# A two-layer graph transformer on one core: the bias rows move from accumulating transfers to VectorE, x is loaded once per graph, and the order of all pieces is laid anew

## The chip, the cores and the metric

The kernel runs on one core of one Trainium2 chip. The metric is the device time of one execution in microseconds (us), lower is better. The kernel before takes 3296.09 us as the median of three runs (3287.92 to 3308.08). A second set of numbers comes from one profiled execution: the hardware profiler's record of every instruction and every DMA packet. That execution took 3294.25 us, and its span from the first to the last instruction is 3292.5 us.

## The reference

For each of 32 graphs there is `x` (512 nodes x 256 features, float32) and `adj` (512 x 512, int32). Two layers follow each other, cut here to what matters:

```python
def _L0_gnn_ref(x, adj, ...):
    allowed = (adj > 0) | (jnp.swapaxes(adj, 1, 2) > 0) | eye
    q, k, v = heads of x @ Wqkv.T + bqkv               # 8 heads of 32
    attn = softmax(where(allowed, q * scale @ k.T, -inf))
    x = _layernorm(x + (attn @ v) @ Wo.T + bo, ln1_g, ln1_b)
    ff = relu(x @ W1.T + b1) @ W2.T + b2               # 1024 hidden
    return _layernorm(x + ff, ln2_g, ln2_b)

x = _layernorm(x + _L0_gnn_ref(x, adj, ...), axis=-1)  # layer 0
x = _layernorm(x + _L1_gnn_ref(x, adj, ...), axis=-1)  # layer 1: mask adj != 0, attention, Wo, no MLP
```

All matrices of weights stay in SBUF. The sums that a softmax divides by are taken over 512 keys for each of 8 heads and 512 queries.

## The kernel before

Each graph is an object of class `Graph`, and the work on it is cut into small pieces, each a method that issues one to eight instructions. The nodes lie on the 128 partitions in four chunks. A piece is named here as in the code, with its layer and its index: `scores(1, 3)` is the score matmul of layer 1 for head group 0 (four heads) and key chunk 3, `scores(1, 7)` the one of head group 1 and key chunk 3.

**The order is written out by hand.** Five graphs, `a` to `e`, are in work at the same time. `opening` (L578) starts the first ones, `period` (L1421) is run 26 times, each time one graph further on, and `closing` (L1737) finishes the last ones. Under `tc.manual_schedule()` every engine takes its pieces in just this order; a piece waits by semaphores for what it needs. In one `period`, `a` ends layer 1, `b` is in the second norm and layer 1, `c` in layer 0's sums and MLP, `d` in layer 0's scores, `e` is being loaded. Each queue is in order: a DMA that has to wait on SP holds back all DMAs behind it on SP, and likewise on POOL.

**Attention.** `scores` (TensorE), `exp` (ScalarE), `masked` (VectorE, multiplies by the mask, L410) and `product` (TensorE, with `v`) run for eight k per layer. Each `p(layer, k)` holds 128 keys x 4 heads x 512 queries. The sums of `p` over the keys take this chain, for each head group:

- `pair` (L430, POOL queue): an accumulating DMA adds one `p` tile of 1 MB onto its neighbour.
- `fold` (L433, VectorE): adds the partial sums of key chunks into one tile, `p(layer, 2)` or `p(layer, 3)`.
- `halve` (L438, POOL queue): two accumulating DMAs add partitions 64 to 127 onto 0 to 63 (`P // 2`, 512 KB), then 32 to 63 onto 0 to 31 (`P // 4`, 256 KB); the second waits for the first to land.
- `spread` (L443, SP queue): four DMAs of 64 KB bring the four heads under one another into the tile `part`.
- `blocks` (L471), `reduce` (L477), `invert` (L480), `widen` (L488), `divide` (L492), all on VectorE: transpose, last sum, reciprocal, and the scaling of the context `cT`.

`project` (TensorE) multiplies `cT` by Wo, `add` (L512, VectorE) adds the residual. `stats`, `aggregate`, `root` (POOL, two instructions, L523 and L524), `center`, `affine` (VectorE) and `norm` (ScalarE, L544) are the norms; `hidden`, `relu`, `mlp` the MLP. TensorE writes dense results into PSUM tiles that share three buffers (tag `d`).

**x and the biases.** `load` (L278, SP) brings x of a graph into the tile `x`, 512 KB, and `again` (L281, SP) brings it a second time into `x1`. `bias` (L323) adds a row that is the same for all nodes, three times per graph, each by an accumulating DMA of 512 KB on the POOL queue from SBUF to SBUF: `bias(1)` adds `bov[0]` to `x1`, the residual of layer 0's attention; `bias(0)` adds `be2` to `x`, the residual behind the MLP's norm; `bias(2)` adds `bov[1]` to `x2`, the residual of layer 1.

**The next graph's x, transposed.** `flip` (L336, SP) is a DMA transpose of half a graph's x from HBM into the `v` tile, `sort` (L341, SP) moves its 16-bit halves to their places, `join` (ScalarE, L348) puts them together. `entries` (L290) and `entry` (L293) load the adjacency and its transpose from a bfloat16 copy that `cast` (POOL queue, L284) makes.

The pieces around the sums of layer 1's head group 0 stand so in `period` before:

```python
b.fold(1, 2, 2, 0)
...
b.halve(1, 0, P // 2)
...
e.flip(0); b.bias(2); e.flip(1); e.sort(1, 0, 0)
...
b.halve(1, 0, P // 4); b.spread(1, 0, 1); b.halve(1, 1, P // 2); c.bias(0)
...
b.spread(1, 0, 2); b.halve(1, 1, P // 4); e.sort(0, 1, 0); d.pair(0, 0); b.spread(1, 0, 0); d.pair(0, 2)
b.spread(1, 0, 3); b.blocks(1, 0); b.reduce(1, 0); c.mlp(0); c.hidden(1, 4); c.add(2, 0)
```

Of the kernel before, what the change touches and what calls it, by code (L numbers as in the profile page):

```python
# [14 lines left out]
ALU = mybir.AluOpType  # L15
# [12 lines left out]
def kernel(ctx: ExitStack, tc: tile.TileContext, t: dict, out: bass.AP):  # L28
# [12 lines left out]
    nc = tc.nc  # L41
    x, adj = t["x"], t["adj"]
    B, N, D = x.shape
# [107 lines left out]
    def plain(pools: ExitStack):  # L151
# [35 lines left out]
        class Graph:  # L187
# [6 lines left out]
            def at(self, tag, n, shape, dtype=F32, **kw):  # L194

                key = (tag, n)
                if key not in self.tiles:
                    name = f"{tag}_{self.b}" + ("" if n is None else f"_{n}".replace(", ", "_").strip("()"))
                    pool = small if tag in SMALL else ps_s if tag == "s" else ps_a if tag == "acc" else work
                    self.tiles[key] = pool.tile([P, *shape], dtype, tag=tag, name=name, **kw)  # L200
                return self.tiles[key]
# [78 lines left out]
            def again(self):  # L280
                nc.sync.dma_start(out=self.x1, in_=x[self.b].rearrange("(c p) d -> p c d", p=P))  # L281

# [36 lines left out]
            def bias(self, i):  # L319

                row = (be2, *bov)[i]
                dst = self.x if i == 0 else self.x1 if i == 1 else self.x2
                nc.gpsimd.dma_start(out=dst, in_=row[:, None, :].to_broadcast([P, NQ, D]), accum_op=ALU.add)  # L323
# [254 lines left out]
        def opening(a, b, c, d, e):  # L578

            a.load()  # L580
            a.transpose(0, 1)
            a.transpose_out(0, 1)
            a.transpose(0, 0)
            a.cast()
            a.transpose_out(0, 0)
            a.constants(0, 4)
            a.query_key(0, 1, 0, None)
            a.query_key_out(0, 1, 0, None)
            b.flip(0)
            b.sort(0, 1, 0)  # L590
            a.entries()
            a.entry(1)
            a.query_key(0, 0, 0, None)
            a.query_key_out(0, 0, 0, None)
            a.query_key(0, 1, 1, None)
            a.scores(0, 1)
            a.exp(0, 1)
            a.entry(2)
            a.entry(3)
            a.value(0, 0)  # L600
            a.scores(0, 0)
            a.entry(0)
            a.exp(0, 0)
            a.query_key(0, 0, 1, None)
            a.query_key_out(0, 0, 1, None)
            a.query_key_out(0, 1, 1, None)
            a.masks(0)
            a.scores(0, 2)
            a.exp(0, 2)
# [3 lines left out]
            a.value(0, 1)  # L613
            a.value_out(0, 1)
            a.again()
            a.constants(10, 12)
            a.masked(0, 1)
            a.masked(0, 2)
            a.scores(0, 3)
            a.masks(3)  # L620
            a.value_out(0, 0)
            a.product(0, 0)
            a.exp(0, 3)
            b.cast()
            b.flip(1)
            a.constants(22, 23)
            a.scores(0, 4)
            a.masked(0, 3)
            a.exp(0, 4)
            a.masked(0, 4)  # L630
            a.scores(0, 6)
            a.exp(0, 6)
            a.pair(0, 0)
            a.product(0, 1)
            a.product(0, 2)
            a.pair(0, 2)
            b.sort(0, 0, 0)
            a.constants(8, 10)
            b.sort(0, 1, 1)
            a.scores(0, 5)  # L640
            a.exp(0, 5)
            a.masked(0, 5)
            a.product(0, 3)
            a.context(0, 0)
            a.masked(0, 6)
            b.sort(1, 0, 0)
            a.fold(0, 2, 2, 0)
            a.product(0, 4)
            a.pair(0, 4)
            b.sort(0, 0, 1)  # L650
            b.join(0, 0)
            b.sort(1, 1, 0)
            b.sort(1, 1, 1)
            a.scores(0, 7)
            a.product(0, 5)
            a.product(0, 6)
            a.exp(0, 7)
            a.masked(0, 7)
            a.constants(4, 6)
            b.join(1, 1)  # L660
            b.sort(1, 0, 1)
            b.join(1, 0)
            b.join(0, 1)
            a.once(0)
            b.query_key(0, 0, 0, None)
            b.query_key(0, 1, 0, None)
            b.query_key_out(0, 1, 0, None)
            b.query_key_out(0, 0, 0, None)
            b.scores(0, 3)
            b.exp(0, 3)  # L670
            a.halve(0, 0, P // 2)
            a.halve(0, 0, P // 4)
            b.entry(0)
            a.product(0, 7)
            a.spread(0, 0, 0)
            a.spread(0, 0, 3)
            b.scores(0, 0)
            b.exp(0, 0)
            b.query_key(0, 1, 1, None)
            b.query_key_out(0, 1, 1, None)  # L680
            b.entries()
            a.context(0, 1)
            a.spread(0, 0, 1)
            a.fold(0, 3, 6, 7)
            a.fold(0, 3, 3, 4)
            b.scores(0, 2)
            b.exp(0, 2)
            b.value(0, 0)
            a.halve(0, 1, P // 2)
            a.halve(0, 1, P // 4)  # L690
            a.spread(0, 0, 2)
            a.blocks(0, 0)
            a.reduce(0, 0)
            a.invert(0, 0)
            a.spread(0, 1, 0)
            a.spread(0, 1, 2)
            a.spread(0, 1, 1)
            a.widen(0, 0)
            b.scores(0, 1)
            b.exp(0, 1)  # L700
            b.query_key(0, 0, 1, None)
            a.spread(0, 1, 3)
            b.query_key_out(0, 0, 1, None)
            b.value_out(0, 0)
            b.scores(0, 5)
            a.divide(0, 0)
            a.blocks(0, 1)
            b.value(0, 1)
            b.exp(0, 5)
            a.reduce(0, 1)  # L710
            a.invert(0, 1)
            a.widen(0, 1)
            a.divide(0, 1)
            a.project(0, 0)
            a.constants(6, 8)
            a.once(2)
            a.bias(1)
            a.add(1, 0)
            a.add(1, 1)
            c.cast()  # L720
            a.stats(1, 0)
            b.entry(2)
            b.entry(3)
            a.stats(1, 1)
            a.project(0, 1)
            b.value_out(0, 1)
            a.aggregate(1, 0)
            a.aggregate(1, 1)
            a.root(1, 0, 2)
            b.entry(1)  # L730
            c.flip(0)
            a.center(1, 0)
            a.affine(1, 0)
            a.center(1, 1)
            a.guard(0, 0, 0)
            a.affine(1, 1)
            b.masks(0)
            b.masks(1)
            c.sort(0, 1, 0)
            a.transpose(1, 0)  # L740
            a.transpose_out(1, 0)
            b.scores(0, 6)
            a.hidden(0, 6)
            b.exp(0, 6)
            a.hidden(0, 0)
            a.relu(0, 1)
            a.add(1, 3)
            a.add(1, 2)
            a.relu(0, 0)
            b.load()  # L750
            a.hidden(0, 2)
            a.constants(12, 14)
            a.bias(0)
            a.relu(0, 3)
            a.hidden(0, 4)
            b.masks(2)
            a.relu(0, 2)
            b.masked(0, 2)
            a.relu(0, 4)
            b.masked(0, 0)  # L760
            b.scores(0, 4)
            b.masked(0, 1)
            a.stats(1, 2)
            b.product(0, 0)
            b.pair(0, 0)
            b.masked(0, 3)
            b.product(0, 1)
            a.stats(1, 3)
            b.product(0, 2)
            b.exp(0, 4)  # L770
            a.aggregate(1, 3)
            b.product(0, 3)
            b.pair(0, 2)
            a.aggregate(1, 2)
            a.root(1, 2, 4)
            a.center(1, 2)
            a.affine(1, 2)
            a.relu(0, 6)
            a.relu(0, 7)
            a.relu(0, 5)  # L780
            a.mlp(1)
            a.center(1, 3)
            a.affine(1, 3)
            a.transpose(1, 1)
            b.masked(0, 5)
            a.add(2, 1)
            a.stats(2, 1)
            a.constants(17, 20)
            a.mlp(0)
            b.masked(0, 4)  # L790
            a.add(2, 0)
            a.aggregate(2, 1)
            a.stats(2, 0)
            a.aggregate(2, 0)
            a.transpose_out(1, 1)
            a.hidden(1, 0)
            a.constants(14, 17)
            a.constants(20, 22)
            a.hidden(1, 6)
            c.sort(0, 1, 1)  # L800
            a.center(2, 0)
            a.root(2, 0, 2)
            b.context(0, 0)
            a.relu(1, 1)
            a.affine(2, 0)
            a.center(2, 1)
            a.relu(1, 6)
            a.affine(2, 1)
            b.masked(0, 6)
            a.relu(1, 7)  # L810
            c.flip(1)
            c.sort(1, 1, 0)
            a.hidden(1, 4)
            a.hidden(1, 2)
            c.sort(0, 0, 0)
            b.scores(0, 7)
            a.relu(1, 5)
            a.stats(3, 1)
            a.aggregate(3, 1)
            a.relu(1, 2)  # L820
            c.sort(0, 0, 1)
            a.guard(0, 1, 0)
            a.guard(0, 1, 1)
            a.stats(3, 0)
            b.product(0, 4)
            a.relu(1, 0)
            d.cast()
            a.aggregate(3, 0)
            b.pair(0, 4)
            a.relu(1, 3)  # L830
            a.relu(1, 4)
            a.mlp(3)
            b.fold(0, 2, 2, 0)
            b.halve(0, 0, P // 2)
            b.exp(0, 7)
            b.masks(3)
            a.root(3, 0, 2)
            b.masked(0, 7)
            a.add(2, 3)
            a.stats(2, 3)  # L840
            a.aggregate(2, 3)
            a.center(2, 3)
            a.offset(3, 0, 2)
            a.norm(3, 1)
            a.root(2, 3, 4)
            a.affine(2, 3)
# [2135 lines left out]
```

## Time and profile before

| what | value |
|---|---|
| median of three runs | 3296.09 us |
| profiled execution, its own time | 3294.25 us |
| its span | 3292.5 us |
| granted TensorE clock, mean | 0.961 |
| TensorE (PE) busy | 3032.3 us, 92% |
| VectorE (DVE) busy | 2652.7 us, 81% |
| ScalarE (ACT), GpSimd (POOL) busy | 1760.1 us, 1149.4 us |
| stores of a graph (L576), from 1022.7 to 2531.7 us | 16, so 100.6 us per `period` |

A row of a timeline gives the start, the duration in us, the engine, the line, the operation and its tiles, and in brackets how long the engine had been idle and which event ended that. `p_(1_2_10336` is the tile `p(1, 2)` of a graph, the last number tells buffers apart. "SPq" is a DMA issued on SP; the duration of such a row is that of the issue, not of the transfer. In the view by stretches each engine's busy time is followed by its number of instructions, and behind these stand the granted clock, the mean busy share of the 16 DMA engines (over 1 where packets overlap) and GB/s.

### The profile page before, as it was taken

The page shows a single profiled execution, that of the slowest core. Times are in us where ns is not written, and L with a number is a line of the kernel's source. Part 1 is how long each engine was busy: PE and PEld are TensorE (multiplying, and loading weights), DVE is VectorE, ACT ScalarE, POOL GpSimd, SP SyncE. Part 2 cuts the span into 40 slices and gives each one's busy share as a digit, 9 for nine tenths or more (in the row PEclk, how much of TensorE's full clock was granted, in tenths as well). Part 3 has the DMA queues.
Part 4 walks back from the last instruction along what each step waited for, and adds up shares of the span by engine and source line. Part 5 has one row for each costly group of instructions (what it writes and reads, how often), then busy time and mean ns, then how long its engine had stood idle before and what let it go on. Part 6 is the DMA issues. An engine that isn't in the chain of part 4 may idle for free.

```text
span 3292.5 us, 43923 instructions
## 1 busy us (share of the span) xinstructions
PE 3032.3 (92%) x16242; PEld 1758.3 (53%) x16242; DVE 2652.7 (81%) x3556; ACT 1760.1 (53%) x2111; POOL 1149.4 (35%) x1474
## 2 busy tenths in 40 slices
PE   6998999999999999998999999999999999999988
PEld 2654555555555555555555555555555555555454
DVE  4687988888978888887789778788888897878876
ACT  4445555555655555555556554565555555555543
POOL 1232433343433333323334333343333333343332
PEclk9899999999999999999999999999999999999999
DMA  8898989998888998898988899888999888898862
GB/s 180 145 168 143 161 165 163 173 173 157 159 159 163 175 173 141 158 168 162 173 151 157 161 164 175 157 154 162 164 170 175 161 150 159 162 179 151 154 125 53
DMA packets 364767, 521.93 MB, mean 159 GB/s; under 512 B 161473, under 2 KB 311105, under 8 KB 327745
## 3 DMA queue, kind: packets, MB, share of 16 engines
q0 software_dynamic: 95056, 364.42, 65.5%
q1 hardware_dynamic: 269488, 154.63, 20.9%
q8 instruction: 130, 2.13, 0.3%
q14 instruction: 93, 0.75, 0.1%
HBM read 89.01 MB, written 33.55 MB: 37 GB/s over the span
## 4 chain that ended last, share of the span: by engine, by line
DVE 33%; PE 29%; DMA 16%; SPq 7%; issue 7%; ACT 5%; POOL 2%; DVEq 0%; POOLq 0%; ACTq 0%
SPq L443 5%; PE psF L571 4%; PE psQK_None L383 4%; PE psH L555 3%; PE psO L501 3%; PE psQK L383 3%; PE psV L371 2%; SPq L341 2%; POOL rs L524 1%; PE psT L358 1%; DVE mv L518 1%; POOL rs L523 1%; ACT x L544 1%; DVE x L541 1%; DVE cT L492 1%
## 5 line engine op out<-in xcount | busy, mean ns | idle before, releaser
L555 PE MATMUL psH<-xT,w_L_gnn_W 128*128 128x256 f32 x2048 | 513.3, 411 | 139.7 <-DVE y_(2_0_8655 L512 9.6
L555 PEld LDWEIGHTS psH<-xT,w_L_gnn_W 128*128 128x128 f32 x2048 | 418.6, 207 | 244.1 <-ACT cT L426 20.5
L523 POOL TENSOR_SCALAR rs<-mv 128x2 f32<-128x2 f32 (+1 forms) x320 | 275.2, 860 | 720.1 <-DVE mv L518 694.7
L565 ACT ACTIVATE hT<-psH,c_L_gnn_b 128x256 f32<-128x256 f32 x512 | 217.8, 473 | 468.2 <-PE psH L555 464.1
L571 PE MATMUL psF<-w_L_gnn_W,hT 128*128 128x256 f32 x2048 | 463.8, 382 | 0.0
L571 PEld LDWEIGHTS psF<-w_L_gnn_W,hT 128*128 128x128 f32 x2048 | 381.5, 190 | 95.7 <-ACT hT L565 43.7
L524 POOL TENSOR_TENSOR rs<-rs,neg_half 128x2 f32<-128x2 f32 (+1 forms) x320 | 283.5, 886 | 26.9
L501 PE MATMUL psO<-w_L_gnn_Wo,cT 128*128 128x256 f32 x1024 | 251.7, 400 | 33.4 <-DVE cT L492 33.4
L383 PE MATMUL psQK_None<-xT,w_L_gnn_Wqkv 128*128 128x512 f32 x512 | 243.9, 609 | 4.7 <-DMA w_L_gnn_Wqkv<-in_L_gnn_Wqkv_dram 4.7
L501 PEld LDWEIGHTS psO<-w_L_gnn_Wo,cT 128*128 128x128 f32 x1024 | 202.8, 202 | 84.1 <-DVE cT L492 36.6
L383 PEld LDWEIGHTS psQK_None<-xT,w_L_gnn_Wqkv 128*128 128x128 f32 x512 | 92.6, 191 | 133.8 <-issue 109.4
L358 PEld LDWEIGHTS psT<-ident,x 128*128 128x128 f32 x520 | 59.7, 144 | 129.8 <-ACT x L544 83.0
L371 PE MATMUL psV<-w_L_gnn_Wqkv,xT 128*128 128x256 f32 x512 | 127.4, 392 | 0.0
L358 PE MATMUL psT<-ident,x 128*128 128x128 f32 x520 | 89.6, 292 | 40.3 <-ACT x L544 33.0
L371 PE MATMUL psV<-w_L_gnn_Wv,xT 128*128 128x256 f32 x512 | 124.4, 386 | 0.0
L371 PEld LDWEIGHTS psV<-w_L_gnn_Wqkv,xT 128*128 128x128 f32 x512 | 92.2, 189 | 58.0 <-issue 25.2
L371 PEld LDWEIGHTS psV<-w_L_gnn_Wv,xT 128*128 128x128 f32 x512 | 92.5, 190 | 36.5 <-issue 26.5
L363 ACT COPY xT<-psT 128x512 f32<-128x512 f32 x130 | 75.1, 578 | 60.7 <-PE psT L358 60.7
L323 POOL DMA_DIRECT2D x<-bov x64 | 98.1, 1532 | 3.2 <-PE psT L358 2.1
L348 ACT COPY xT<-kT 128x512 uint16<-128x512 uint16 x124 | 94.2, 765 | 7.0 <-DMA kT<-v 4.7
L389 ACT ACTIVATE qT<-psQK_None,c_L_gnn_bqkv 128x512 f32<-128x512 f32 x64 | 43.9, 688 | 74.0 <-PE psQK_None L383 74.0
L376 ACT COPY v<-psV 128x512 f32<-128x512 f32 x128 | 73.9, 581 | 11.7 <-PE psV L371 11.6
(6836 smaller groups left out, 6570.3 us busy)
## 6 DMA issues: line engine op xcount, KB each, us to landing
x<-in_x_dram SPq DMA_DIRECT2D x64, 512.0 KB, 4.5
x<-bov POOLq DMA_DIRECT2D x64, 512.0 KB, 8.0
code<-in_adj_dram POOLq DMA_DIRECT2D x32, 512.0 KB, 6.6
m<-code SPq DMA_DIRECT2D x32, 512.0 KB, 13.1
x<-s_L_gnn_ln_b POOLq DMA_DIRECT2D x32, 512.0 KB, 9.1
out_dram<-x SPq DMA_DIRECT2D x32, 512.0 KB, 4.6
kT<-v SPq DMA_DIRECT2D x248, 64.0 KB, 5.7
m<-code SPq DMA_TRANSPOSE x128, 4.1
```

Of the source, the lines that this page charges most:

```text
L323: nc.gpsimd.dma_start(out=dst, in_=row[:, None, :].to_broadcast([P, NQ, D]), accum_op=ALU.add)
L348: nc.scalar.copy(words[:, :, h * 2 * P : (h + 1) * 2 * P, w], self.sorted(h)[:, w * ND : (w + 1) * ND, :])
L358: nc.tensor.transpose(ps[:, c, j * P : (j + 1) * P], src[:, 2 * h + j, c * P : (c + 1) * P], ident)
L371: nc.tensor.matmul(ps[:, j, :], xT[:, i, at], proj[layer][0][2][:, i, :], start=(i == 0), stop=(i == ND - 1))
L383: nc.tensor.matmul(ps, w[:, i, c * P : (c + 1) * P], xT[:, i, at], start=(i == 0), stop=(i == ND - 1))
L443: nc.sync.dma_start(out=part[j * HD : (j + 1) * HD, :], in_=self.p(layer, 2 + hg)[:HD, j, :])
L501: nc.tensor.matmul(ps[:, j, :], self.cT(layer)[:, k, at], wo[layer][:, k, :], start=(k == 0), stop=(k == ND - 1))
L523: nc.gpsimd.tensor_scalar(rs, self.mv(n)[:, a:b, 1:2], EPS, None, ALU.add)
L524: nc.gpsimd.tensor_tensor(rs, rs, neg_half[:, a:b, None], ALU.pow)
L555: nc.tensor.matmul(ps[:, j, :], w1[:, c, at], xT[:, c, h * 2 * P : (h + 1) * 2 * P], start=(c == 0), stop=(c == ND - 1),)
L565: nc.scalar.activation(self.hT(h)[:, f, :], ps[:, f % 2, :], AF.Relu, bias=b1[:, f : f + 1])
L571: nc.tensor.matmul(ps, self.hT(h)[:, f, j * P : (j + 1) * P], w2[:, f, :], start=(f == 0), stop=(f == NF - 1))
```

## The change

`again` is gone and `bias` becomes one VectorE instruction on 128 partitions x 1024 elements with the row broadcast. `bias(1)` now writes `x1` from `x`, so x is read from HBM once by `load` (the transposed copy through `flip` stays). A helper also names tiles in another way.

```diff
-            def again(self):
-                nc.sync.dma_start(out=self.x1, in_=x[self.b].rearrange("(c p) d -> p c d", p=P))
...
             def bias(self, i):
 
-                row = (be2, *bov)[i]
+                row = (be2, *bov)[i][:, None, :].to_broadcast([P, NQ, D])
                 dst = self.x if i == 0 else self.x1 if i == 1 else self.x2
-                nc.gpsimd.dma_start(out=dst, in_=row[:, None, :].to_broadcast([P, NQ, D]), accum_op=ALU.add)
+                nc.vector.tensor_tensor(dst, self.x2 if i == 2 else self.x, row, ALU.add)
```

`opening`, `period` and `closing` hold new lists. `period` has the same pieces as before without `again`, in another order and cut at another point of the cycle. Its two DMA queues now read, from the start of the list to its end:

```
SP:   a.spread(1,1,1) a.spread(1,1,0) a.spread(1,1,2) d.sort(0,1,1) d.sort(0,0,0) d.entries d.sort(1,0,1)
      d.load d.sort(1,1,1) d.entry(0) d.entry(2) d.sort(0,0,1) c.spread(0,0,0) c.spread(0,0,2)
      c.spread(0,0,1) c.spread(0,0,3) c.spread(0,1,3) c.spread(0,1,0) c.spread(0,1,2) c.spread(0,1,1)
      d.entry(3) e.entry(1) e.flip(1) e.sort(1,0,0) b.spread(1,0,3) e.flip(0) e.sort(1,1,0) b.spread(1,0,2)
      b.spread(1,0,1) b.spread(1,0,0) e.sort(0,1,0) a.store b.spread(1,1,3)
POOL: c.pair(0,0) b.root(3,0,2) c.pair(0,2) b.root(2,3,4) b.root(3,3,4) b.root(2,2,3) b.root(3,2,3)
      c.halve(0,0,64) b.guard c.pair(0,4) c.halve(0,0,32) c.halve(0,1,64) a.guard a.root(4,2,4) a.root(4,0,2)
      b.guard c.halve(0,1,32) e.cast b.pair(1,0) b.pair(1,2) c.root(1,0,2) c.guard a.guard a.guard b.pair(1,4)
      c.root(1,2,4) b.halve(1,0,64) b.halve(1,0,32) b.halve(1,1,64) b.halve(1,1,32) c.guard b.guard
      c.root(2,0,2)
```

The stretch of the new `period` from layer 1's folds over its end into the next one, where `b` becomes `a`, `c` becomes `b` and `d` becomes `c`:

```python
b.fold(1, 2, 2, 0)
...
d.masks(0); c.affine(1, 2); c.center(1, 3); c.affine(1, 3); b.halve(1, 0, P // 2)
b.fold(1, 3, 6, 7); b.fold(1, 3, 3, 4); b.halve(1, 0, P // 4); b.halve(1, 1, P // 2); b.halve(1, 1, P // 4)
b.product(1, 7); d.masked(0, 0); c.mlp(1); c.add(2, 1); d.masked(0, 1); c.mlp(0); c.add(2, 0)
...
e.flip(1); e.sort(1, 0, 0); b.spread(1, 0, 3); e.flip(0); d.masked(0, 3); e.sort(1, 1, 0)
b.spread(1, 0, 2); d.masked(0, 2); b.spread(1, 0, 1); b.spread(1, 0, 0); b.blocks(1, 0); b.reduce(1, 0)
...
e.sort(0, 1, 0); c.root(2, 0, 2); a.store(); c.affine(2, 0); b.spread(1, 1, 3); d.product(0, 1)
# the next period
a.divide(1, 0); b.affine(2, 1); a.spread(1, 1, 1); a.spread(1, 1, 0); c.product(0, 2); c.pair(0, 0)
a.spread(1, 1, 2); a.blocks(1, 1); b.mlp(3); c.masked(0, 5); a.reduce(1, 1); c.pair(0, 2)
...
a.widen(1, 1); b.mlp(2); c.product(0, 3); a.divide(1, 1); a.project(1, 0)
```

In the middle of the new list, where layer 0's sums end: `c.fold(0, 3, 3, 4)`, `c.bias(0)`, two halves and four spreads, `c.blocks(0, 1)` to `c.divide(0, 1)`, then `c.project(0, 0)`. `b.bias(2)` stands just ahead of that fold, `d.bias(1)` between `b.masked(1, 6)` and `b.fold(1, 2, 2, 0)`.

## The prediction

> **What bounds the kernel now.** I began with the page's busy shares, went on to VectorE's timeline of one `period` (1522 to 1623 us) for its idle times, then to POOL's and SP's timelines for the chain behind the largest of them, and last to stretches of 5 us for the clock.
>
> ```profile
> span 3292.5 us, 43923 instructions
> PE 3032.3 (92%) x16242; PEld 1758.3 (53%) x16242; DVE 2652.7 (81%) x3556; ACT 1760.1 (53%) x2111; POOL 1149.4 (35%) x1474
> q0 software_dynamic: 95056, 364.42, 65.5%
> q1 hardware_dynamic: 269488, 154.63, 20.9%
> ```
>
> TensorE is nearly full; the two DMA queues together keep the 16 engines busy 86% of the time, q0 being all that POOL issues. TensorE's own work per period, from start-to-start times in its timeline: 16 `scores` of 1.07, 16 `product` of 0.95, 8 `hidden` of 1.79, 4 `mlp` of 3.6, 4 `project` of 1.81, 4 `value` of 1.83, 6 full and 4 half `query_key` of 1.82 and 0.93, 4 `transpose` of 0.55: **92.4 us**. The period takes 100.6. The missing 8.2 us are mostly one place:
>
> ```profile
> 1592.53 0.88 POOL L438 DMA_DIRECT2D p_(1_2_10336<-p_(1_2_10336  x1
> 1593.15 1.63 POOL L323 DMA_DIRECT2D x<-bov  x1
> 1600.19 0.88 POOL L438 DMA_DIRECT2D p_(1_2_10336<-p_(1_2_10336  x1 [2.97 <-DMA p_(1_2_10336<-p_(1_2_10336]
> 1604.81 1.33 POOL L323 DMA_DIRECT2D x<-s_L_gnn_ln_b  x1 [1.35 <-issue]
> 1605.91 3.00 SPq L443 DMA_DIRECT2D part_(1_0_10583<-p_(1_2_10336  x2
> 1610.85 3.46 SPq L443 DMA_DIRECT2D part_(1_0_10583<-p_(1_2_10336  x2
> 1621.73 0.71 DVE L471 STREAM_TRANSPOSE sT_(1_0_10663<-part_(1_0_10583 128x512 f32<-128x512 f32 x1 [9.73 <-DMA part_(1_0_10583<-p_(1_2_10336]
> ```
>
> The chain of layer 1's first head group takes 29.2 us from its first `halve` (1592.53) to `blocks` (1621.73), and VectorE stands 9.73 us before `blocks`. `add(2, 0)` stands behind that and frees a PSUM buffer, so TensorE stops too. Both adding rows of `bias` lie inside the chain. What the stretches show of the same place:
>
> ```profile
> 1607.00:1612.00 5.00, 5.00 (x40) 2.61 (x33) 4.86 (x8) 3.58 (x4) 2.05 (x4) 1.00 1.07 169
> 1612.00:1617.00 5.00, 5.00 (x25) 4.41 (x24) 0.01 (x1) 1.74 (x4) 0.73 (x1) 1.00 0.97 145
> 1617.00:1622.00 5.00, 0.48 (x3) 0.08 (x1) 0.27 (x1) 0.84 (x2) 0.00 (x0) 0.75 1.04 209
> 1622.00:1627.00 5.00, 3.14 (x7) 2.52 (x8) 3.65 (x8) 0.00 (x0) 1.34 (x4) 0.50 1.02 181
> ```
>
> TensorE is idle from 1617, the DMA share is 0.97 to 1.07, and after the stop the granted clock is 0.50 for a while: 16 `hidden` matmuls that take 3.62 us elsewhere took 5.11 at 1524.53, behind the same stop. So a stop costs its length and about 1.5 us more.
>
> On this the Trainium skill has a rule (TensorE: Matmul & The Clock Gate, What's actually happening): after an idle window of about 3.4 us the array drops to half rate until it has been busy as long. The row agrees. By the rule a stop of 6 us split into two of 3 would save the 1.5 us; the sum below takes no such saving.
>
> **VectorE's own account** decides the rest. Its work per period: 16 `masked` and 6 `fold` of 2.2, four each of `blocks`, `reduce`, `widen`, `divide` of 0.70, four `invert` of 0.25, `masks` 3.0, 12 `add` and 16 `stats` and 8 `center` of 0.43, 8 `affine` of 0.46, 16 `aggregate` of 0.15, 5 `offset` of 0.13: 85.8 us. Its idle times in that period's timeline: 9.73 at `blocks`, 1.36 for an `exp`, and 1.15, 1.16, 0.94, 0.27 for `root`: 14.6. Together 100.4, the period.
>
> **The change, part by part.** (1) *Three bias adds on VectorE.* No row shows a 128x1024 float32 add. `fold`, with two float32 inputs in SBUF, takes 2.29 for 2048 elements, `divide` 0.69 for 512; between them 1.0 to 1.4, and I take half a `fold`, 1.17. Three make 3.5 us: VectorE 89.3 us of work beside TensorE's 92.4. None of the three waits: x2's transposes and x's load are over 10 us earlier in the new order. At full cover they cost nothing; without cover 3.5 x 26 = 91 us.
>
> The row that speaks against them: `root`'s second instruction has a median of 0.72 us (L524) but took 2.65 at 1533.90, inside a `masked` from 1533.69 to 1535.98. A bias add could hold one `root` by at most its 1.17. In the new order `halve` or `pair` follow each of them on POOL rather than a `root`, so I take 0, with 3.5 per period as the other end. The Trainium skill (SBUF, Who interferes with whom) says just that: a VectorE instruction with two SBUF inputs keeps a GpSimd instruction that reads SBUF waiting until it ends. By its rule alone the three adds would cost POOL up to their whole length, by the order nothing on the path.
>
> (2) *Three accumulating transfers and one load go.* q0 takes 0.655 x 3292.5 = 2157 us for 364.42 MB, 5.9 us per MB; three of 0.524 MB are 9.3 us of the DMA engines' time per period, and `again` at q1's 4.4 us per MB 2.3. These are estimates. The period's DMA load falls from about 0.89 x 100.6 = 89.5 to 78 us. POOL loses three issues of 1.5 us, SP one of 0.6; neither is full. What this buys is shorter landings: a 512 KB `halve` took 5.5 us from issue to landing in layer 0's second group (view of DMA issues for 1520 to 1625) and 7.4 in layer 1's first, four `spread` 2.6 against 7.3.
>
> (3) *The order.* I measure it by the work that each engine has between two pieces of the new list, in the durations above. Two places are tight.
>
> Place one, **layer 0's second group**. From the end of `fold(0,3,3,4)` to `blocks(0,1)` VectorE has 14.1 us of work and some 1.2 idle for a `root`. In the old trace the same chain went from 1556.83 to the last landing at about 1573.8: 17.0 us. So VectorE waits about 1.7 there, and `project(0,0)`, which follows `divide(0,1)` closely, makes TensorE wait about 2 (between 0, if VectorE is ahead, and 4).
>
> Place two, **layer 1's sums**. Let F be the end of `fold(1,2,2,0)`. `halve` 64 and 32: F+11 by layer 0's landings (5.5 and 4.8, plus issues), F+14 by layer 1's old ones. On SP `spread(1,0,3)`, then `flip(0)` with an issue of 2.7 us, a `sort`, three more `spread` (0.65 each when nothing holds them): F+17 to F+20, landing 2.6 us later. VectorE has 19.2 us of work up to `blocks(1,0)`, so it waits 0 to 4 there. The second group's spreads are behind `sort(0,1,0)`, and that waits for `flip(0)` to land (8.2 us after its issue, L336's median): F+20 to F+23, then `store` and four `spread`, landing at F+25 to F+30. VectorE reaches `blocks(1,1)` at F+25.4 plus what it waited before. `project(1,0)` needs VectorE to have finished 12.0 us of the new list when TensorE has done 11.8. From `project(0,0)` to there TensorE has 53.8 us, VectorE 52.6: only 1.2 to spare. With 0.7 of `root` waits and about 3 at the two `blocks`, TensorE waits 2.5 (0 to 7). `add(2,0)` no longer stands behind `blocks(1,0)`: the old stop is gone, and this is what is late next.
>
> **The sum.** 92.4 + 2.0 + 2.5 + 0.6 for a clock that dips now and then = 97.5 us per period against 100.6: 26 x 3.1 = 81 us less. VectorE's account agrees: 89.3, 1.7 and 3 at `blocks`, about 3 for `root`, 0.5 for TensorE. `opening` and `closing` have TensorE lists of the same length to 2 us; they stop in many places (3080 to 3100 has 13.5 busy of 20) and closing gets 17 us more VectorE work beside idle VectorE. I take 0, with 25 either way. 3294.25 - 81 = **3213 us**; the profiled execution lies 2 us under the median of the runs.
>
> **Rivals.**
>
> *TensorE runs through* (B). For it: DMA load falls 13%, and spreads landed in 2.6 us where the engines were less busy. Against it: a flip now sits among the spreads. The period is 92.4 to 94: 26 x 7.3 = 190 less, 3104.
>
> *The wait only changes places* (C). For it: in the trace SP stood 6.8 us before a `sort` until a flip had landed, and such a pair now stands ahead of each group of spreads. If the spreads keep landing in 7 us, the two `blocks` cost VectorE 6 instead of 3 and the period is about 100: 3280.
>
> *VectorE becomes the bound* (D, slower). Place: `blocks(1,0)` and `blocks(1,1)` behind flips and sorts on SP. VectorE has 89.3 us of work; once its idle time is over 11.3 us per period, against 14.6 now, it alone makes the period longer than 100.6. If the whole 14.6 stays, the period is 103.9: 26 x 3.3 = 86 more, 3380. Against it: the bias transfers that shared the chain's stretch are gone.
>
> *The change not doing what it says*: that the order gives nothing by itself and the transfers alone count is inside C.
>
> **How the numbers follow.** Forecast (3150 to 3265) 0.45, B 0.15, C 0.20, D 0.20. The range leaves out the lower half of B and most of D: 3100 to 3330. A measurement of this kernel tells about 1% (33 us) from no change. Faster by over 1%: the forecast, B and a little of C, 0.63; within 1%: most of C, 0.16; slower: D and a remainder, 0.21.
>
> **What would show it.** Stores 97 to 98 us apart. On VectorE no wait over 5 us; `blocks` waits of 1 to 4 at (1,0), (1,1) and (0,1). TensorE waiting at `project` (L501) for `divide` (L492), no longer at `hidden` (L555) for `add` (L512). Bias adds of 1.0 to 1.4 us. DMA share at 0.80 to 0.85. I would be wrong if landings stayed at 7 us, if SP's sorts held the spreads longer than one flip, or if some tile's buffer is now reused so early that a DMA waits for its last reader.

## The result, and the profile after

The changed kernel takes **3405.22 us** (median of four runs, 3402.22 to 3416.09); the kernel before, on the same chip, 3292.65 us (3287.92 to 3308.08). The ratio is **1.034, 95% interval 1.030 to 1.038**: slower, where 3213 was forecast. The profiled execution took 3408.14 us, its mean granted clock is 0.951 (0.961 before). The stores of 16 graphs in the middle of the trace are 104.7 us apart, before 100.5 by the same count. 26 periods of 4.2 us make 109 of the 114 us by which the two profiled executions differ.

The first lines of the page of the changed kernel, its two DMA queues, and two of its costliest groups (number of instructions, then busy time and mean ns of one, then the idle time ahead of the group and what ended most of it):

```profile
span 3406.4 us, 43921 instructions
...
PE 3041.2 (89%) x16242; PEld 1762.2 (52%) x16242; DVE 2764.9 (81%) x3652; ACT 1734.3 (51%) x2111; POOL 1002.4 (29%) x1378
...
q0 software_dynamic: 44368, 314.08, 54.2%
q1 hardware_dynamic: 252592, 137.85, 17.7%
...
L498 PE MATMUL psO<-w_L_gnn_Wo,cT 128*128 128x256 f32 x1024 | 308.8, 456 | 250.0 <-DVE cT L489 249.5
...
L468 DVE STREAM_TRANSPOSE sT<-part 128x512 f32<-128x512 f32 x126 | 89.1, 707 | 322.7 <-DMA part<-p 320.8
```

The two queues carry 67 MB less, as they should, and the engines are less busy with them (72% of a longer span against 86%). TensorE now waits mainly in one group, the matmuls of `project` (now L498): 250 us, for `divide` (L489). VectorE lost 323 us ahead of `blocks` (L468), waiting for `spread`. In the kernel before, `project` (L501) and `hidden` (L555) stood so:

```profile
L501 PE MATMUL psO<-w_L_gnn_Wo,cT 128*128 128x256 f32 x1024 | 251.7, 400 | 33.4 <-DVE cT L492 33.4
L555 PE MATMUL psH<-xT,w_L_gnn_W 128*128 128x256 f32 x2048 | 513.3, 411 | 139.7 <-DVE y_(2_0_8655 L512 9.6
```

The stop at `hidden` is gone, as was forecast (1.8 us of idle time on the new page), but the new one at `project` is larger, and the matmuls of `project` are slower (456 ns on the mean, 400 before). One period of the timeline shows where. L435 is `halve`, L281 `cast`, L440 `spread`, L427 `pair`:

```profile
1611.62 0.82 POOL L435 DMA_DIRECT2D p<-p  x1 [7.89 <-DVE p L430]
...
1617.22 0.87 POOL L435 DMA_DIRECT2D p<-p  x1 [0.40 <-DMA p<-p]
1617.83 0.81 POOL L281 DMA_DIRECT2D code<-in_adj_dram  x1
...
1621.97 6.52 SPq L440 DMA_DIRECT2D part<-p  x4
...
1625.23 0.90 POOL L427 DMA_DIRECT2D p<-p  x1 [6.59 <-DMA part<-p]
1626.94 0.87 POOL L427 DMA_DIRECT2D p<-p  x1 [0.81 <-PE acc L414]
...
1635.92 0.71 DVE L468 STREAM_TRANSPOSE sT<-part 128x512 f32<-128x512 f32 x1 [9.56 <-DMA part<-p]
...
1639.30 5.00 PE L498 MATMUL psO<-w_L_gnn_Wo,cT 128*128 128x256 f32 x14 [8.41 <-DVE cT L489]
...
1678.66 0.71 DVE L468 STREAM_TRANSPOSE sT<-part 128x512 f32<-128x512 f32 x1 [0.65 <-DMA part<-p]
```

This is layer 0's second group. Its four spreads, issued in 2.4 us where nothing holds them, take SP 6.5 us; 3.73 of these are the second one's issue alone. They land 4.71, 8.38, 7.46 and 8.78 us after their issues, the last at 1635.84. The same four in the trace of before:

```profile
1567.88 3.33 SPq L443 DMA_DIRECT2D part_(0_1_10373<-p_(0_3_9959  x4
```

They had landed 2.0 to 3.5 us after their issues, the last at 1572.61, beside one `bias` transfer (issued 1563.77, landing 1571.14). What is new beside them is `e.cast` (issued 1617.83, landing 8.63 us later) and then `b.pair(1, 0)` and `b.pair(1, 2)` (landing 8.35 and 12.62 us after their issues). In the old list `e.cast` stood at the start of the period, and the first of the two pairs was issued (1573.62) when the last spread had landed. The last row of the period above (1678.66) is layer 1's first group, where VectorE waited 9.73 us before: it now waits 0.65. The stop has moved from one group of sums to another.

The stretches of the same place (VectorE's column is the third):

```profile
1629.00:1634.00 5.00, 1.89 (x6) 0.76 (x4) 0.00 (x0) 2.93 (x3) 0.00 (x0) 1.00 1.02 200
1634.00:1639.00 5.00, 0.00 (x0) 0.00 (x0) 2.81 (x5) 0.00 (x0) 0.00 (x0) 0.70 0.87 172
1639.00:1644.00 5.00, 4.70 (x14) 3.81 (x14) 4.08 (x7) 0.00 (x0) 0.00 (x0) 0.62 0.03 7
```

While VectorE and then TensorE stand, the DMA engines are full (1.02, 0.87); when the second pair has landed too, 3.7 us behind the last spread (1639.57), they are empty (0.03). TensorE comes back at a granted clock of 0.62.

### The profile page after: what moved, and what is told of

The parts are those of the page before. It is cut to its first block, busy times and chain, and to the rows that moved or that the text cites. A ratio compares the mean times of both kernels' runs of the same rounds, so it can differ in the third digit from the quotient of the medians.

```text
span 3406.4 us, 43921 instructions
## 1 busy us (share of the span) xinstructions
PE 3041.2 (89%) x16242; PEld 1762.2 (52%) x16242; DVE 2764.9 (81%) x3652; ACT 1734.3 (51%) x2111; POOL 1002.4 (29%) x1378
## 4 chain that ended last, share of the span: by engine, by line
PE 52%; DVE 17%; DMA 15%; issue 6%; SPq 5%; ACT 3%; POOL 2%; DVEq 0%; POOLq 0%; ACTq 0%
PE psH L552 12%; DMA part<-p 10%; PE psF L568 10%; PE s L394 9%; PE acc L414 7%; PE psO L498 7%; DVE p L407 6%; DMA p<-p 5%; SPq L440 5%; DVE p L430 3%; ACT p L403 3%; PE psQK_None L380 2%; PE psV L368 2%; PE psT L355 2%; PE psQK L380 1%
## 5 line engine op out<-in xcount | busy, mean ns | idle before, releaser
L403 ACT ACTIVATE p<-s 128x2048 f32<-128x2048 f32 x512 | 961.3, 1878 | 707.6 <-PE s L394 481.1
L407 DVE TENSOR_TENSOR p<-p,m 128x2048 f32<-128x2048 f32 x512 | 1155.5, 2276 | 59.1 <-ACT p L403 59.0
L394 PE MATMUL s<-qT,kT 32*128 32x512 f32 x4096 | 591.2, 647 | 84.1 <-ACT p L403 75.2
L498 PE MATMUL psO<-w_L_gnn_Wo,cT 128*128 128x256 f32 x1024 | 308.8, 456 | 250.0 <-DVE cT L489 249.5
L414 PE MATMUL acc<-p,v 128*32 128x512 f32 x4096 | 491.8, 601 | 1.6 <-ACT cT L423 1.2
L435 POOL DMA_DIRECT2D p<-p x252 | 212.2, 845 | 861.3 <-DVE p L430 445.6
L430 DVE TENSOR_TENSOR p<-p,p 128x2048 f32<-128x2048 f32 x189 | 430.8, 2280 | 3.7 <-DMA p<-p 2.0
L520 POOL TENSOR_SCALAR rs<-mv 128x2 f32<-128x2 f32 (+1 forms) x320 | 167.6, 524 | 791.1 <-DVE mv L515 781.8
L498 PEld LDWEIGHTS psO<-w_L_gnn_Wo,cT 128*128 128x128 f32 x1024 | 231.4, 234 | 320.9 <-DVE cT L489 261.6
L394 PEld LDWEIGHTS s<-qT,kT 32*128 32x128 f32 x4096 | 161.3, 184 | 369.5 <-ACT p L403 162.9
L468 DVE STREAM_TRANSPOSE sT<-part 128x512 f32<-128x512 f32 x126 | 89.1, 707 | 322.7 <-DMA part<-p 320.8
L427 POOL DMA_DIRECT2D p<-p x189 | 172.4, 913 | 526.8 <-PE acc L414 219.7
L414 PEld LDWEIGHTS acc<-p,v 128*32 128x32 f32 x4096 | 109.5, 109 | 327.8 <-issue 249.4
L521 POOL TENSOR_TENSOR rs<-rs,neg_half 128x2 f32<-128x2 f32 (+1 forms) x320 | 260.7, 815 | 26.8
L512 DVE BATCH_NORM_STATS2 st<-y 128x6 f32<-128x256 f32 x384 | 159.1, 422 | 7.2
```

The source lines that it names most:

```text
L394: nc.tensor.matmul(s[:, j, :], self.kT(layer)[at, hg, kc * P : (kc + 1) * P], self.qT(layer)[at, hg, :], start=True, stop=True,)
L403: nc.scalar.activation(self.p(layer, k), self.at("s", (layer, k), [HPC, N]), AF.Exp, scale=SCALE)
L407: nc.vector.tensor_tensor(p, p, m[:, k % NQ, None, :].to_broadcast([P, HPC, N]), ALU.mult)
L414: nc.tensor.matmul(acc[j * HD : (j + 1) * HD, :], self.v(layer)[:, kc, h * HD : (h + 1) * HD], self.p(layer, k)[:, j, :], start=(kc == 0), ...
L430: nc.vector.tensor_tensor(self.p(layer, dst), self.p(layer, a), self.p(layer, b), ALU.add)
L435: nc.gpsimd.dma_start(out=p[:rows], in_=p[rows : 2 * rows], accum_op=ALU.add)
```

## The experiments

Three theories stood at the start. **Theory 1**: the new order puts `cast`, and then two pairs, beside the spreads of layer 0's second group, on the same DMA engines. **Theory 2**: VectorE, with three adds more, has become the bound. **Theory 3**: the new order as a whole leaves the chains too little time. All ratios are to the kernel before, run on the same chip; the last column is the mean of 16 distances between stores in the middle of one profiled execution.

| run | median us | ratio, 95% interval | us per period |
|---|---|---|---|
| the change | 3405.22 | 1.0339 (1.0296 to 1.0382) | 104.7 |
| cast_late | 3176.53 | 0.9639 (0.9589 to 0.9688) | 96.1 |
| pairs_late | 3312.23 | 1.0060 (1.0038 to 1.0082) | 100.7 |
| no_bias_add | 3370.68 | 1.0233 (1.0188 to 1.0279) | 104.0 |
| old_order_vector_bias | 3215.49 | 0.9765 (0.9708 to 0.9822) | 98.2 |
| old_order_cast_beside | 3217.75 | 0.9767 (0.9727 to 0.9806) | 98.2 |
| new_order_transfer_bias | 3531.77 | 1.0735 (1.0687 to 1.0784) | 108.0 |
| cast_early | 3359.34 | 1.0194 (1.0153 to 1.0235) | 103.0 |
| cast_behind_pairs | 3167.65 | 0.9645 (0.9619 to 0.9672) | 95.3 |
| cast_late_bias1_late | 3131.40 | 0.9488 (0.9446 to 0.9529) | 95.0 |
| casts_late_all | 3110.04 | 0.9487 (0.9440 to 0.9533) | 92.7 |

### One piece moved: the cast

```diff
             c.halve(0, 1, P // 4)
-            e.cast()
...
             c.root(1, 0, 2)
+            e.cast()
```

> The changed kernel with one piece moved in `period`: `e.cast` from behind `c.halve(0,1,32)` to behind `c.root(1,0,2)`, where the trace shows the DMA engines idle (share 0.01 to 0.03). Theory 1, collision on the DMA engines: the four spreads of layer 0's second group share the engines with `cast` and then with two `pair` of 1 MB, so that they land 8.8 us after their issue and not 2.6; without `cast` their issue takes 3.3 us in place of 5.1 and they land 3 to 6 us earlier. TensorE's wait at `project(0,0)` falls from about 9 us to 3 to 6 per period, the time from 3405 to 3260 to 3330. Theory 2, VectorE is the bound with its 3.6 us more work: no change, 3390 to 3410. Theory 3, the order alone leaves the chain of halves and spreads too little time, whatever the engines do: at most 1 us per period, 3380.

It took **3176.53 us**, 229 us less than the change, more than theory 1 had said. The waits between 600 and 2800 us of the changed kernel (total us, number of waits, longest):

```profile
PE psO L498 <- DVE cT L489: 189.8, 22, 12.7
...
DVE sT L468 <- DMA part<-p: 226.9, 40, 13.8
```

and of this one:

```profile
PE s L394 <- ACT p L403: 64.5, 47, 4.7
PE psO L498 <- DVE cT L489: 3.8, 3, 2.2
...
DVE sT L468 <- DMA part<-p: 19.7, 22, 3.4
```

The wait at `project` is all but gone, and the wait at `blocks` with it. The timeline of the same chain:

```profile
1505.48 0.82 POOL L435 DMA_DIRECT2D p<-p  x1 [7.52 <-DVE p L430]
...
1511.50 0.87 POOL L435 DMA_DIRECT2D p<-p  x1 [0.82 <-DMA p<-p]
...
1516.23 2.78 SPq L440 DMA_DIRECT2D part<-p  x4
...
1519.09 0.89 POOL L427 DMA_DIRECT2D p<-p  x1 [6.71 <-DVE p L407]
...
1520.48 0.71 DVE L468 STREAM_TRANSPOSE sT<-part 128x512 f32<-128x512 f32 x1 [0.26 <-DMA part<-p]
```

The four issues take 2.78 us in all, and they are over before the first pair is issued, though the pairs have kept their place in the list. From the end of `fold(0, 3, 3, 4)` (1505.19) to the last landing (1520.40) the chain takes 15.2 us; in the changed kernel the same chain took 24.5 (1611.32 to 1635.84). Theory 3 falls with this as it was put: the order as a whole stays, and one piece moved gives back all that was lost and more.

### The other neighbours: the two pairs

```diff
-            b.pair(1, 0)
-            b.pair(1, 2)
...
             c.root(1, 0, 2)
+            b.pair(1, 0)
+            b.pair(1, 2)
```

> The changed kernel with `b.pair(1,0)` and `b.pair(1,2)` moved in `period` from ahead of the second group's spreads to behind `c.root(1,0,2)`; `cast` stays. Theory 1 (collision): the spreads land after 3 to 5 us, not 8.8, TensorE's wait at `project(0,0)` falls from 9 to about 3 or 4 per period, but `fold(1,2,2,0)` then may wait a few us for the second pair: 3250 to 3340. Theory 2 (VectorE): no change. Theory 3 (order alone): no change or slower, since layer 1's chain starts later.

3312.23 us. The cast is where the change has it, and the second spread's issue still takes 3.3 us (1677.80 in this trace), but the third and fourth, issued behind it, now land in 2.0. The chain takes 18.4 us (1665.45 to 1683.85). Its waits, 600 to 2800 us:

```profile
PE s L394 <- ACT p L403: 100.6, 55, 5.0
PE psO L498 <- DVE cT L489: 43.1, 22, 2.5
...
DVE sT L468 <- DMA part<-p: 99.3, 44, 3.7
DVE p L430 <- DMA p<-p: 88.1, 25, 5.0
```

So the delay has two links. The cast holds back one issue on SP by about 3 us; the pairs are issued meanwhile, and beside them the last three spreads need 7 to 9 us in place of 2 to 5. Taking the second link away costs something new here: the folds wait 88 us for pairs that are now late (last row).

### Is VectorE the bound?

The three adds are left out, so the output lacks the three bias rows:

```diff
-                nc.vector.tensor_tensor(dst, self.x2 if i == 2 else self.x, row, ALU.add)
+                return
...
-                    r = self.x1 if n == 1 else self.x2
+                    r = self.x if n == 1 else self.x2
```

> The changed kernel without the three bias adds: the rows are left out of the computation, `add` of layer 0's attention reads x itself. VectorE has 3.6 us less work per period. Theory 2 (VectorE is the bound): the whole 3.6 x 26 = 95 us go, 3310. Theories 1 and 3 (the wait for the spreads sets the period): only the add that stands ahead of `fold(0,3,3,4)` starts the chain earlier, 1.2 us per period, about 30 us: 3375.

3370.68 us, 34.5 less than the change, where theory 1 had said some 30 and theory 2 had said 95. By the stores the period is 104.0: of 3.66 us of VectorE work, 0.7 came back. TensorE waits as long as ever for `divide`:

```profile
PE psO L498 <- DVE cT L489: 198.1, 22, 12.6
```

Theory 2 falls for the changed kernel. In the changed kernel's period VectorE's idle times in the timeline add up to 15.5 us and its work to the other 89.1, but 9.56 of the idle time is the wait for the spreads.

### The transfers alone, in the old order

Before's lists with the VectorE add and one load; two `bias` pieces in `opening` change places and `closing` loads `d` earlier, so that x is there.

> The kernel before, in its own order, with the bias rows added by VectorE and x loaded once: the first half of the change without the new order (bias keeps its places in the list; for two graphs of `opening` its first two calls are swapped, and one `load` of `closing` takes the place of the second load, so that x1 is made from x before the second row is added to x). Theory 1 (collision): the two bias transfers that ran beside layer 1's chain are gone, the stop of 6.8 us per period shrinks to 2 to 4: 3190 to 3240, so the new order alone cost 170 to 210 us. Theory 2 (VectorE): the added 3.6 us show wholly or in part, 3300 to 3390. Theory 3 gives nothing of its own here: 3290.

3215.49 us: taking the bias and the second load off the DMA engines is worth 2.3% (1.8 to 2.9) with the order left as it was. Beside this run the new order costs 190 us as it was delivered, and it gains 39 with the cast moved (`cast_late`, 3176.53, on the same chip).

### The cast beside the spreads, in the old order

```diff
-            e.cast()
...
             c.halve(0, 1, P // 4)
+            e.cast()
```

> The old order with the bias adds on VectorE (3215.49 us), with one piece moved: e.cast from the start of period to just behind c.halve(0, 1, P // 4), where the new order has it, so beside the four spreads of layer 0's second group; the two pairs of layer 1 stay well behind those spreads. Theory 1 (the transfer of cast holds up the spreads, in any order): the second spread's issue goes from 0.6 to 3-4 us and the last of the four lands 5 to 8 us later than now. But in the old order VectorE reaches blocks(0, 1) 6.4 us after that landing, so most of it is covered: 3215 to 3270. Theory 3 (the new order as a whole is at fault, the cast only a part of it): issues stay at 0.6 and landings at 2.0. If the cast cost its 8 us wherever it stands beside spreads, without regard to cover: 3330 or more.

3217.75 us, no difference. The timelines of POOL, SP and VectorE in this run:

```profile
1534.21 0.79 POOL L281 DMA_DIRECT2D code<-in_adj_dram  x1
...
1538.33 5.75 SPq L440 DMA_DIRECT2D part_(0_1_10357<-p_(0_3_9944  x4
...
1548.70 0.70 DVE L468 STREAM_TRANSPOSE sT_(0_1_10385<-part_(0_1_10357 128x512 f32<-128x512 f32 x1
```

and in the old order without the move:

```profile
1628.82 2.41 SPq L440 DMA_DIRECT2D part_(0_1_11032<-p_(0_3_10619  x4
...
1639.02 0.70 DVE L468 STREAM_TRANSPOSE sT_(0_1_11060<-part_(0_1_11032 128x512 f32<-128x512 f32 x1
```

The first link is there again: the four issues take 5.75 us in place of 2.41, and the last landing is 17.6 us behind the fold's end (1527.83 to 1545.47) in place of 14.5 (1618.14 to 1632.61). But `blocks` comes 20.9 us behind that end in both (no bracket in either row: VectorE didn't wait), and here the pairs are issued only when the spreads have been issued. The new order's list gives the chain some 15 us, the old one 21. The cast's hold on SP is the same in both orders; what it costs is decided by the cover, which is the work that VectorE has meanwhile, and by what POOL issues meanwhile.

### Earlier by one place, later by two

```diff
+            e.cast()
             c.halve(0, 1, P // 4)
-            e.cast()
```

> The new order with e.cast moved by one place only, from just behind c.halve(0, 1, P // 4) to just ahead of it: POOL issues it about 4.5 us earlier, while the first half of the chain is on its way. Theory 1 as it stands (cast against the spreads): the spreads' issues come back to 0.6 us and they land in 2 to 5; the two halves lose some 2 us each; VectorE waits 3 to 7 at blocks(0, 1) in place of 9.6; 3230 to 3340. If what counts is only that the 1.5 MB of the cast and the chain share the engines at some time between fold and blocks: 3390 to 3420, as the changed kernel.

3359.34 us, above what theory 1 had said. POOL's and SP's timelines:

```profile
1600.57 0.64 POOL L281 DMA_DIRECT2D code<-in_adj_dram  x1
1601.19 0.87 POOL L435 DMA_DIRECT2D p<-p  x1
...
1608.20 2.78 SPq L440 DMA_DIRECT2D part<-p  x4
...
1608.73 0.89 POOL L427 DMA_DIRECT2D p<-p  x1 [6.67 <-PE acc L414]
```

SP's issues are free again (2.78), so the hold does belong to the cast. But the second `halve` now lands 6.88 us after its issue, where it took 4.6 alone, and that is enough to bring the last two spreads beside the pair of 1608.73: they land in 7.48 and 8.25 us, and the chain takes 23.4 (1594.83 to 1618.27). From period to period it takes 17.1 to 27.3.

```diff
-            e.cast()
...
             b.pair(1, 2)
+            e.cast()
```

> The changed kernel with e.cast moved by two places on the POOL queue, from ahead of b.pair(1, 0) to behind b.pair(1, 2): still in the same stretch, but issued some 3 us behind the spreads of layer 0's second group in place of 4 us ahead of them. Theory 1, as the last runs narrowed it (the cast holds the second spread's issue on SP for 3 us, and this brings the last two spreads beside the two pairs): issues of 0.6 us, landings of 2 to 3, the wait at blocks(0, 1) gone; only the pairs land later, by at most the cast's own 5 us; 3165 to 3230. If the bytes of cast and pairs in this stretch are what counts, whatever their order: 3300 to 3405.

**3167.65 us**, as good as `cast_late`, with the cast in the same stretch and all the same bytes. The spreads land in 2.0 us and the chain takes 15.0 (median of 16 periods; in the changed kernel the median is 24.6); only the cast itself is slow now, 13.5 us from issue to landing, and nobody waits for it. The bytes in the stretch aren't the cause; which of them stand ahead of the spreads is. Waits of this run, 600 to 2800 us:

```profile
PE s L394 <- ACT p L403: 63.9, 48, 3.9
PE psO L498 <- DVE cT L489: 2.6, 2, 2.3
```

### The accumulating transfers in the new order

`cast_late` with `bias` as three accumulating transfers and `again` in its lists, as in the kernel before.

> The new order with e.cast behind c.root(1, 0, 2) as in the run of 3176.53 us, but with the three bias rows as accumulating transfers on the POOL queue and x loaded a second time (again behind c.spread(0, 1, 1) in period, behind load elsewhere). If the price of the transfers is that of the old order (76 us), about 3252, 3220 to 3290. If the new order leans on VectorE's adds (c.bias(0) now stands between the halves of layer 0's groups, d.bias(1) and b.bias(2) beside folds), over 3290. If the transfers are hidden in this order, 3176 to 3200.

**3531.77 us**, against 3176.53 with the adds: in this order the transfers cost 11%, in the old one 2.4% (1 / 0.9765). POOL's, VectorE's and TensorE's timelines (L323 is `bias`, L438 `halve`, L430 `pair`):

```profile
1546.61 0.89 POOL L430 DMA_DIRECT2D p<-p  x1 [1.46 <-PE acc L417]
1547.19 1.65 POOL L323 DMA_DIRECT2D x<-bov  x1
1548.78 0.90 POOL L438 DMA_DIRECT2D p<-p  x1
1549.31 1.74 POOL L323 DMA_DIRECT2D x<-s_L_gnn_ln_b  x1
1557.05 0.85 POOL L438 DMA_DIRECT2D p<-p  x1 [6.00 <-DVE mv L518]
...
1586.02 0.71 DVE L471 STREAM_TRANSPOSE sT<-part 128x512 f32<-128x512 f32 x1 [11.93 <-DMA part<-p]
...
1589.40 1.22 PE L501 MATMUL psO<-w_L_gnn_Wo,cT 128*128 128x256 f32 x2 [11.26 <-DVE cT L492]
```

Two of the three bias transfers stand among the halves of layer 0, and the halves land 11.84 and 10.04 us after their issues (1548.78, 1557.05) where 4.6 to 5.7 is usual. That delay brings the second group's spreads beside the pairs again: the last two land 8.13 and 10.38 us after their issues. The two parts of the change are no sum of two prices.

### A better version

What was left in `cast_late` is `scores` waiting for `exp`, and `exp` for a `p` buffer that a fold frees. `d.bias(1)` stood ahead of that fold:

```diff
-            d.bias(1)
             b.fold(1, 2, 2, 0)
...
             b.fold(1, 3, 3, 4)
+            d.bias(1)
```

> The kernel of 3176.53 us (cast behind c.root(1, 0, 2)) with d.bias(1) moved from ahead of b.fold(1, 2, 2, 0) to behind b.fold(1, 3, 3, 4): the folds end 1.2 us earlier, and the wait that is left there (TensorE at scores for exp, exp for a buffer that fold frees) gets shorter. Up to 1.2 us per period: 3145 to 3177. If VectorE's work is the bound instead of the order, the same 3177 within 10.

**3131.40 us, 0.949 of the kernel before**, 45 us less than `cast_late` and under the range that was expected. Its page and its wait:

```profile
span 3137.5 us, 43921 instructions
...
PE 2987.6 (95%) x16242; PEld 1730.6 (55%) x16242; DVE 2764.6 (88%) x3652; ACT 1734.4 (55%) x2111; POOL 1020.3 (33%) x1378
```

```profile
PE s L394 <- ACT p L403: 49.0, 48, 3.9
```

In `opening`, too, two casts stand at spreads:

```diff
-            d.cast()
             b.spread(0, 1, 2)
...
             b.root(1, 0, 2)
+            d.cast()
...
-            e.cast()
             c.spread(0, 0, 1)
...
             c.root(1, 0, 2)
+            e.cast()
```

> The kernel of 3131.40 us (cast and bias(1) late in period) with the same done in opening: d.cast from just ahead of b.spread(0, 1, 2) to behind b.root(1, 0, 2), e.cast from ahead of c.spread(0, 0, 1) to behind c.root(1, 0, 2). In opening the spreads beside d.cast land in 9 to 10.4 us, and TensorE stops 8.2 us at the first project behind them. Theory 1: 5 to 14 us less, 3117 to 3127. If opening is held by something else, such as the entries that a later cast delays: 3131 within 6.

The ratio is 0.9487, with an interval that covers the run before it: the two aren't told apart. In its trace TensorE's stop at the first `project` behind `d.cast` is 1.30 us (8.16 without the move), and TensorE is busy 263 of the first 300 us in place of 252, so the local effect is there; the four runs lie 1.4% apart, which hides it. Its `period` holds the same list as the run before, yet its stores are 92.7 us apart on the mean and not 95.0. The medians of the 16 distances nearly agree (92.5 and 93.1): in the trace of the run before, three of the 16 are 102.6 to 104.5 us long, each with two stretches of 3.4 us at a granted clock of 0.50, and the trace of this run has none such. The one trace was also taken in the slowest of four runs (3139.26) and the other in the fastest (3086.36). Why some periods are long, no run shows.

## Why the prediction was wrong

- **Place one is the step that failed.** "In the old trace the same chain went from 1556.83 to the last landing at about 1573.8: 17.0 us. So VectorE waits about 1.7 there." It took 24.5 and VectorE waited 9.56. The old figure was itself a little high: in the old trace the last spread lands at 1572.61, so the chain took 15.8. That error is small and goes the other way. What failed is that the landing was carried from a trace in which the cast stood elsewhere and the pairs came after the spreads. The new POOL list, with `e.cast`, `b.pair(1,0)`, `b.pair(1,2)` right behind `c.halve(0,1,32)`, was laid out in the section on the change, and the prediction priced none of the three. With the cast two places later the chain takes 15.0 and TensorE waits 2.6 us at `project` in 2200 us: the step's reckoning of VectorE's work (15.3 with the wait for `root`, 15.0 measured) holds, and the 2 us that it entered for TensorE are not even needed.
- **Place two was said too dear.** `blocks(1, 0)` was to cost VectorE 0 to 4 and TensorE 2.5; VectorE waited 0.65 in the period shown, TensorE's waits at `project` are those of layer 0 (one of 0.66 us apart), and `flip` landed in 3.2 to 6.1 us (600 to 2800 us, median 4.1), not in the 8.2 taken from the old trace. Same mistake, other sign: a landing belongs to its neighbours.
- **The sum.** 97.5 us per period was forecast; the kernel with the one piece moved has 96.1, and 3176.53 us against 3213. So the loss is one term: 8.4 us of TensorE's time per period at `project(0, 0)`, where 2 had been entered, and a clock that comes back at 0.62 behind the stop. That the rest comes out near is partly luck: in `cast_late` the two waits entered at 2.0 and 2.5 are 0.2 together, and TensorE waits 2.8 per period at `scores` for `exp` (64.5 us in 2200), for which the sum had no term.
- **The adds (1).** 1.22 us each, where 1.17 was taken, and none of them waits. "At full cover they cost nothing" was wrong for one: `bias(1)` ahead of layer 1's folds was on the path, and moving it behind them gave 1.1 us per period by the mean of the stores, 2.3 by their median. Leaving all three out of the changed kernel gave 0.7. The prediction had no `root` beside an add; one is there (L521 at 1654.66, 1.56 us where 0.72 is usual, beside the add of 1654.42), and VectorE has no idle time behind it.
- **The transfers (2).** DMA load per period: 75 us measured (71.9% of 104.7) for 78 estimated. That this "buys shorter landings" was right in kind, and 2.3% in the old order; the share of 0.80 to 0.85 wasn't reached.
- **`opening` and `closing`**: about 5 us more than before, inside the 25 allowed.
- **The rivals.** C had the mechanism, a wait that changes places, but put it at layer 1's groups behind the flips. D had nearly the size (3380), and its arithmetic of VectorE's idle time comes out (15.5 us idle per period, 14.6 before), but its cause is refuted: without the adds the kernel is only 1% faster. B's 92.4 to 94 us per period wasn't reached by the change; the last run's trace, with four pieces moved, has 92.7.

## What to carry to other kernels

A landing time read from a trace holds only beside the transfers that were in flight there: when an order is laid anew, write down for each short transfer on a critical chain what the other queues now issue in the 5 us ahead of it, and price that before any engine's work. Let a large transfer that nobody is waiting for follow the small ones that an engine needs next, not lead them: one line moved by two places was worth 7% here. And price a change of order and a change of what is ordered together: the bias transfers cost 2.4% in one list and 11% in another.

## What the runs showed of the hardware

- A 64 KB `spread` on SP takes 0.6 us to issue and 2.0 to land. Beside a cast of 512 KB issued on POOL about 4 us earlier the second of four issues took 3.3 to 3.9 us in the periods shown, in both orders (2.8 to 5.0 in 21 periods of the changed kernel); beside two accumulating pairs of 1 MB a spread landed in 7.5 to 8.8. On this the Trainium skill (DMA: Bandwidth & Descriptors, Issuing engines are not separate DMA queues) says that transfers run on the same 16 engines and interleave, whichever engine started them. The landings agree; it adds that starting them from several engines saves only the time to issue, and for the second spread not even that was saved. The hold ends about when the cast lands: in the period shown the issue ends at 1626.26 and the cast lands at 1626.45, and over 21 periods the issue ends between 1.2 us ahead of the landing and 0.9 behind it. A `bias` transfer of the same 512 KB, issued 4.1 us ahead of the spreads in the trace of before, held the second issue for only 1.5 us. Why an issue on SP is held, and why the second and not the first, no run here shows.
- The cast is slowed as well: it lands in 5.9 us where `cast_late` has it, in 8.6 beside the spreads and in 13.5 behind the pairs.
- A short stop can cost clock or not. In the changed kernel fourteen matmuls of `project` took 5.00 us behind a stop of 8.41; in `cast_late_bias1_late` they took 3.29 behind one of 2.77 (1596.34). But in `cast_late` a stop of 1.98 us brought the granted clock to 0.50 (view by stretches, 1457 to 1460), and 16 matmuls of `mlp` took 5.00 us in place of 3.62:

```profile
1455.98 1.50 PE L394 MATMUL s<-qT,kT 32*128 32x512 f32 x8 [1.98 <-ACT p L403]
1457.41 5.00 PE L568 MATMUL psF<-w_L_gnn_W,hT 128*128 128x256 f32 x16
```

  So the rule that the prediction quoted, an idle window of about 3.4 us, doesn't tell by the length of a stop alone which one costs clock: by it neither short stop would. What decides it, no run here shows.
